# One core, four blocks in a row: gathers, combining and reflections moved to other places in the instruction order

## The chip, the cores and the metric

The program runs on one core of a Trainium2 chip. The metric is the device time of one execution in microseconds (us), from launch to end, and the figure quoted for a kernel is the median of its runs. A core has five engines that run their own instruction streams in order and meet through semaphores: PE (matrix products), DVE (vector), ACT (scalar functions), POOL (vector work of a slower kind, and all indirect DMA here) and SP (which only starts DMAs in this kernel). A wait of one instruction therefore holds everything that stands behind it on the same engine.

## What is computed

The input x is 4 x 512 x 288 in float32, the condition 4 x 288. Four blocks follow each other: a transformer block whose MLP is a mixture of 4 experts (top 2), a plain transformer block, a rotation in a 64-dimensional subspace, and another plain transformer block. The parts that the change touches come from the first and the third:

```python
# block 0: the expert MLP
topk_logits, topk_idx = jax.lax.top_k(xf @ w_gate, 2)
gates = jax.nn.softmax(topk_logits, axis=-1)
cw = jnp.sum(jax.nn.one_hot(topk_idx, 4) * gates[..., None], axis=1)
hmid = gelu(jnp.einsum('tc,ech->eth', xf, w1) + b1[:, None, :])
eo = jnp.einsum('eth,ehc->etc', hmid, w2) + b2[:, None, :]
x = x + g_mlp[:, None, :] * jnp.einsum('te,etc->tc', cw, eo)
...
# block 2: rotation; it needs only P and the condition until x arrives
U, _ = jnp.linalg.qr(P)                      # P is 288 x 64
R = _rotation(cond, W, b)                    # expm of a 64 x 64 skew matrix per batch
z = jnp.einsum('btn,nd->btd', x, U)
x = x + jnp.einsum('btd,nd->btn', jnp.einsum('btd,bde->bte', z, R) - z, U)
```

## The kernel before

**The order is written out by hand.** Each block is an attention stage followed by an MLP stage. Inside a stage, Python code issues the products of PE one by one, and other work is hung between them: generators are advanced with `next`, and lists of steps are run at fixed places. What is issued earlier stands earlier in each engine's stream. `in_turn(engine, ins)` ties an instruction behind the last one so tied on its engine and takes its place; `take` only takes the place; `beside_of` only ties.

**The expert stage.** Tokens are sorted by expert into 19 items of 256 rows, each the work of one expert (items 0 to 18; item 0 is done at the end of the attention stage). An item has 9 chunks: `hidden` computes four chunks at a time (products of 256 columns into `e0h`, then a gelu on ACT), and `contraction` multiplies by the second weights (two row tiles of 9 products of 288 columns into `e0o`). `others` alternates one group of four chunks with a stretch of the contraction of the item before. Behind each of these steps `breathe()` (L1940) is called once. After a group, `event(i, f)` (L1947) runs what was planned for its chunks.

The weights of an item depend on the sorting, so POOL gathers them by indirect DMA, all through `gathered` (L1815, the instruction of L1818): three first parts (`first_part`, 128 rows of 1,155 floats out of `w1c`), three second parts (`second_part`, 128 rows of 864 floats out of `in_w`, and with the first of them one bias gather), and two gathers of tokens (`tokens_of`). In `finish` (L1953) these are planned per chunk: second part n of item i at chunk n, first part n of item i+1 at chunk 3+n, the tokens of item i+2 at chunks 6 and 7, and at chunk 5 the transposes of item i+1 (`activations`, tile `e0xt`).

From item 12 on, `combining` brings the results of the first two batches back: per tile t of 128 tokens two gathers out of `eo` (`fetched`), two weightings and an addition on DVE, and an addition to x on POOL (L1936). It is planned at chunks, tile t seven chunks after tile t-1. A second list, `self.fine`, holds small pieces of the sorting of the other two batches; `breathe` takes one of them every fourth call.

**The side work.** `tick()` (L772) advances a generator of side work by one step, from the list `beside`; with `both=True` it advances the list `aside` as well, in that order. `beside` starts with `rotation()`: 64 Householder reflections (`reflections`, L579), then 64 steps that build the subspace (`subspace`). `aside` starts with `exponential()` (56 steps: loads and products `psr`, their evacuation `rv`, the matrix `skew`, a Taylor series, 16 squarings `ef`), behind which the modulation of block 1 is put (16 steps, with the tiles `rows` and `psmod`). In an attention stage four ticks fall on each of the 17 rounds; in the expert stage `went` counts the columns that PE streamed and ticks once per `pace` columns, 985 here, with `both`.

One reflection is a chain: on DVE a sum of squares and `n2` (L606), on POOL a square root `nrm` (L609), on DVE six small operations (L614 to L619), then an SP DMA that spreads one row of `pT` over up to 63 partitions (`reflector`, L545, tile `v`), and at last `reflect` on DVE, whose first instruction is the copy of L549. Between them stand the `yield`s, that is, the ticks: after `n2` (L608), after the square root (L610), two after the DMA, and in attention stages one after `reflect`.

## Time and profile before

| | |
|---|---|
| median of 3 runs | 2022.97 us (2016.03, 2022.97, 2024.35) |
| the profiled execution | 2016.98 us |
| its span, first to last instruction | 2015.0 us |
| PE busy | 1913.5 us (95%) |
| DVE, ACT, POOL busy | 1076.7, 746.6, 539.9 us |
| mean granted PE clock | 0.975 |
| attention of block 0, about | 30 to 410 us |
| expert stage, about | 410 to 925 us |
| attention and MLP of block 1, about | 925 to 1460 us |
| rotation, block 3 | 1460 us to the end |

The stages follow from the names of the tiles in the timeline; their bounds are read off where the first and last of these names stand. In the answers quoted below, a line of the waits reads: engine, who waited, for what; total us, how often, the longest. A line of the timeline reads: start us, length us, engine, line, operation, output<-inputs, count, and in brackets the idle time before it and who ended it. A float32 product shows as two records, so x18 stands for nine products.

### The profile page before, as it was taken

What the parts mean: (1) busy time and instruction counts of PE and PEld (TensorE: products, weight loads), DVE (VectorE), ACT (ScalarE), POOL (GpSimd) and SP (SyncE); (2) the same over time, 40 slices, a digit from 0 to 9 for tenths busy, and PEclk for the clock granted to TensorE, in tenths of its full rate; (3) what the DMA queues carried; (4) which work ended last, traced back from release to release, by engine and by line L of the source; (5) the groups of instructions that cost most, each with busy time, mean ns of one, the idle gap of its engine ahead of it and who ended that gap; (6) DMA issues with size and microseconds to landing.
All of it is one profiled execution on the core that took longest, in us unless ns stands there. A gap on an engine that the chain in (4) does not pass through costs nothing. (4 is left out here: it accounts for less than half of the span.)

```text
span 2015.0 us, 28809 instructions
## 1 busy us (share of the span) xinstructions
PE 1913.5 (95%) x10602; PEld 1008.9 (50%) x10602; DVE 1076.7 (53%) x3129; ACT 746.6 (37%) x1367; POOL 539.9 (27%) x776
## 2 busy tenths in 40 slices
PE   7999999998889899899999999999999999999998
PEld 4434443365556667675334443456554344433555
DVE  5666777623434333446777777454155666554211
ACT  1554555332211222232555544511124555555220
POOL 4111121443233445652332122211400211213101
PEclk9999999898889999899999999999999999999999
DMA  7521121346444665651111111220000111111000
GB/s 155 118 54 21 22 45 46 106 117 195 138 138 148 197 203 179 187 183 37 42 44 38 36 37 40 56 61 21 21 1 10 28 29 36 28 26 23 19 15 24
DMA packets 95166, 147.27 MB, mean 73 GB/s; under 512 B 33267, under 2 KB 72798, under 8 KB 95026
## 3 DMA queue, kind: packets, MB, share of 16 engines
q1 hardware_dynamic: 68690, 66.16, 14.3%
q0 software_dynamic: 26224, 79.27, 13.2%
q8 instruction: 84, 1.38, 0.3%
q14 instruction: 56, 0.46, 0.1%
q10 hardware_dynamic: 112, 0.01, 0.0%
HBM read 114.66 MB, written 20.54 MB: 67 GB/s over the span
## 5 line engine op out<-in xcount | busy, mean ns | idle before, releaser
L875 DVE TENSOR_REDUCE max<-a3m 128x1 f32<-128x512 f32 x256 | 164.6, 685 | 128.1 <-PE a3s L78 120.8
L78 PE MATMUL e0h<-e0hT,e0w 128*128 128x256 f32 (+1 forms) x1026 | 213.6, 416 | 13.1 <-DMA e0w<-w1c,wrow 10.2
L875 DVE TENSOR_REDUCE max<-a0m 128x1 f32<-128x512 f32 x256 | 165.3, 683 | 90.2 <-PE a0s L78 78.1
L875 DVE TENSOR_REDUCE max<-a1m 128x1 f32<-128x512 f32 x256 | 165.7, 684 | 75.3 <-PE a1s L78 68.0
L887 ACT ACTIVATE a0p<-a0s 128x512 f32<-128x512 f32 x256 | 140.2, 596 | 144.5 <-PE a0s L78 144.1
L887 ACT ACTIVATE a1p<-a1s 128x512 f32<-128x512 f32 x256 | 140.9, 596 | 139.4 <-PE a1s L78 139.2
L887 ACT ACTIVATE a3p<-a3s 128x512 f32<-128x512 f32 x256 | 140.0, 596 | 137.6 <-PE a3s L78 137.6
L78 PEld LDWEIGHTS e0h<-e0hT,e0w 128*128 128x128 f32 (+1 forms) x1026 | 149.6, 196 | 70.0 <-issue 47.2
L78 PE MATMUL e0o<-e0w,e0hm 128*128 128x288 f32 x648 | 178.6, 427 | 0.1
L78 PE MATMUL a0m<-a0qk,a0qk 32*128 32x512 f32 x512 | 159.1, 645 | 7.9 <-DVE max L875 6.8
L78 PE MATMUL a1m<-a1qk,a1qk 32*128 32x512 f32 x512 | 157.5, 640 | 7.8 <-DVE max L875 6.5
L78 PE MATMUL a0s<-a0qk,a0qk 32*128 32x512 f32 x512 | 161.0, 653 | 0.0
L78 PE MATMUL a1s<-a1qk,a1qk 32*128 32x512 f32 x512 | 158.4, 640 | 0.2 <-DVE u L549 0.2
L78 PE MATMUL a3m<-a3qk,a3qk 32*128 32x512 f32 x512 | 151.2, 643 | 6.8 <-DVE max L875 5.5
L78 PE MATMUL a3s<-a3qk,a3qk 32*128 32x512 f32 x512 | 153.0, 644 | 0.3 <-DVE a3qk L929 0.3
L78 PEld LDWEIGHTS e0o<-e0w,e0hm 128*128 128x128 f32 x648 | 125.5, 198 | 37.3 <-issue 2.7
L1281 ACT ACTIVATE e0hm<-e0h,e0w 128x256 f32<-128x256 f32 x162 | 75.6, 473 | 181.6 <-PE e0h L78 138.8
L609 POOL TENSOR_TENSOR nrm<-n,phalf 64x1 f32<-64x1 f32 (+31 forms) x64 | 36.4, 569 | 321.6 <-DVE n L606 296.4
L78 PEld LDWEIGHTS a1m<-a1qk,a1qk 32*128 32x128 f32 x512 | 46.9, 183 | 73.2 <-DVE max L875 41.1
L78 PEld LDWEIGHTS a0m<-a0qk,a0qk 32*128 32x128 f32 x512 | 47.3, 184 | 69.2 <-DVE max L875 41.2
L549 DVE COPY v<-v 63x1 f32<-63x1 f32 (+62 forms) x63 | 8.8, 139 | 134.5 <-DMA v<-pT 122.0
L78 PE MATMUL f1h<-f1hT,w 128*128 128x512 f32 (+1 forms) x216 | 79.9, 614 | 0.4 <-ACT f1hT L504 0.4
(496 smaller groups left out, 3241.1 us busy)
## 6 DMA issues: line engine op xcount, KB each, us to landing
eo<-e0r SPq DMA_DIRECT2D x50, 144.0 KB
ada<-in_ada SPq DMA_DIRECT2D x18, 324.0 KB
wr<-in_wrot SPq DMA_DIRECT2D x16, 288.0 KB
g<-gates SPq DMA_DIRECT2D x24, 144.0 KB
xm<-e0m SPq DMA_DIRECT2D x6, 576.0 KB
w1c<-in_w SPq DMA_DIRECT2D x20, 144.0 KB
w<-in_w SPq DMA_DIRECT2D x6, 432.0 KB
x<-in_x SPq DMA_DIRECT2D x16, 144.0 KB
```

Of the source, the lines that this page charges most:

```text
L78: ins = nc.tensor.matmul(*args, **kwargs).ins
L549: beside_of("DVE", nc.vector.tensor_copy(v[0:n, 0:1], v[0:n, C - k : C - k + 1]))
L609: in_turn("POOL", nc.gpsimd.tensor_tensor(nrm, n2, phalf[0:n], ALU.pow))
L875: take("DVE", nc.vector.tensor_reduce(m[:, t, i, D : D + 1], ps, AX.X, ALU.max))
L887: take("ACT", nc.scalar.activation(p, ps, AF.Exp, scale=D**-0.5))
L1281: nc.scalar.activation(self.hms[i][f], ps[r][:, 0 : self.width], func, bias=b1(f)),
```

## The change

Four edits, all in the order of issue; no arithmetic and no transfer is added or taken away.

1. In `reflections`, the `yield` between `n2` and the square root and the one after `reflect` in attention stages are removed: a reflection takes three ticks in every stage, where it took five in an attention stage and four in the expert stage.
2. In the expert stage `pace` is 1500 columns, where it was 985.
3. The gathers of an item form one list, made behind chunk 0: tokens of item i+1 (for two items only), the first parts of item i+1, the second parts of item i, the tokens of item i+2. `breathe` takes one behind every third call. What must be there by chunk 5 is taken at once then, the rest at chunk 8.
4. The combining is put into `self.fine`: a list made behind chunk 0 of item 12, with five steps of four `breathe`s to a tile.

```diff
@@ reflections
             nc.vector.tensor_scalar(sgn, alpha, 0.0, 2.0, ALU.is_ge, ALU.mult)
-            yield
             in_turn("POOL", nc.gpsimd.tensor_tensor(nrm, n2, phalf[0:n], ALU.pow))
             yield
...
                 reflect(k, pT, v, n - 1)
-                if inside[0]:
-                    yield
@@ Experts
-        pace, both = 985, True
+        pace, both = 1500, True
...
-        def breathe(self, every=4):
+        def breathe(self):
             self.since += 1
-            if self.fine and self.since >= every:
-                self.since = 0
+            if self.gathers and self.since % 3 == 0:
+                self.gathers.pop(0)()
+            if self.fine and self.since % 4 == 0:
                 self.fine.pop(0)()
@@ finish
-            tokens(2, 1, 1)
+            def gather(i):
+                self.gathers = []
+                if i + 1 in (2, NF0):
+                    self.gathers += self.tokens_of(i + 1)
+                if i < last:
+                    for n in range(FW):
+                        self.gathers.append(lambda n=n: self.first_part(i + 1, n))
+                for n in range(FW):
+                    self.gathers.append(lambda n=n: self.second_part(i, n))
+                self.urgent = len(self.gathers) - FW
+                if i + 2 <= last and i + 2 != NF0:
+                    two = []
+                    self.gathers += [
+                        lambda: (two.extend(self.tokens_of(i + 2)), two[0]()),
+                        lambda: two[1](),
+                    ]
+                self.later = len(self.gathers) - self.urgent
+            def gathered(left):
+                while len(self.gathers) > left():
+                    self.gathers.pop(0)()
             for i in range(1, self.items):
-                for n in range(FW):
-                    at(i, n, lambda i=i, n=n: self.second_part(i, n))
-                    if i < last:
-                        at(i, FW + n, lambda i=i, n=n: self.first_part(i + 1, n))
-                if i + 2 <= last and i + 2 != NF0:
-                    tokens(i + 2, i, 6)
+                at(i, 0, lambda i=i: gather(i))
+                at(i, 5, lambda: gathered(lambda: self.later))
+                at(i, 8, lambda: gathered(lambda: 0))
...
-            tokens(NF0, NF0 - 1, 0)
-            for t in range(HT):
-                k = (NS + 1) * NF + 2 + 7 * t
-                at(*divmod(k, NF), lambda t=t: self.fetched(0, t))
-                steps = combining(0, t)
-                for f, step in zip((6, 7, 8), steps):
-                    at(*divmod(k + f, NF), step)
+            def combine():
+                steps = [[] for _ in range(5 * HT + 4)]
+                for t in range(HT):
+                    steps[5 * t].append(lambda t=t: self.fetched(0, t))
+                    for k, step in zip((4, 5, 7), combining(0, t)):
+                        steps[5 * t + k].append(step)
+                self.fine = [lambda some=some: both(*some) for some in steps]
+            at(NS + 1, 0, combine)
+            at(last - 1, 4, placed)
```

Here NF = 9 chunks, FW = 3, NS = 11, NF0 = 5, HT = 8 and `last` = 18.

More of the change, by code (lines that the diff above doesn't have):

```diff
@@ L1438, in __init__ @@
             self.eo = [kept(f"eo{h}", [n * SW, C]) for h, n in enumerate((NS, NS1))]
-            self.fine, self.since = [], 0
+            self.fine, self.gathers, self.since = [], [], 0
             def pair(tag, shape, dtype=F32):
@@ L1982, in finish @@
             last = self.items - 1
-            def tokens(i, where, f):
-                steps = []
-                at(where, f, lambda: (steps.extend(self.tokens_of(i)), steps[0]()))
-                at(where, f + 1, lambda: steps[1]())
             for n, load in enumerate(loads):
                 at(NS // 2 + n, 4, load)
-            tokens(2, 1, 1)
-            for i in range(1, self.items):
-                for n in range(FW):
-                    at(i, n, lambda i=i, n=n: self.second_part(i, n))
-                    if i < last:
-                        at(i, FW + n, lambda i=i, n=n: self.first_part(i + 1, n))
-                if i + 2 <= last and i + 2 != NF0:
-                    tokens(i + 2, i, 6)
+            def gather(i):
[18 more added lines that the diff above has]
+                    self.gathers.pop(0)()
+            for i in range(1, self.items):
+                at(i, 0, lambda i=i: gather(i))
+                at(i, 5, lambda: gathered(lambda: self.later))
+                at(i, 8, lambda: gathered(lambda: 0))
                 if i < last:
```

## The prediction

> **What bounds the kernel.** I read the page first, then the waits of PE by stage, then the timeline around the long ones.

> ```profile
> PE 1913.5 (95%) x10602; PEld 1008.9 (50%) x10602; DVE 1076.7 (53%) x3129; ACT 746.6 (37%) x1367; POOL 539.9 (27%) x776
> ...
> PE   7999999998889899899999999999999999999998
> ...
> PEclk9999999898889999899999999999999999999999
> ```

> PE sets the time, and where it falls short (slices 8 to 17, 50 us each) its clock is low too. From the granted clock and PE's busy stretches I summed both over the expert stage (430 to 935 us): PE idle 48.7 us, and 30.1 us lost where it ran at half clock. That, 79 us, is all the change can win there. By part, idle + clock: 36.8 + 22.4 up to 700 us, while `aside` still works, and 11.9 + 7.7 after it. The waits of 420 to 930 us:

> ```profile
> POOL nrm L609 <- DVE n L606: 160.2, 35, 15.5
> ...
> DVE v L549 <- DMA v<-pT: 120.8, 30, 10.0
> ...
> PE e0h L78 <- DMA e0w<-w1c,wrow: 10.2, 3, 4.5
> ...
> POOL e0w L1818 <- PE e0o L78: 8.3, 3, 4.8
> ...
> PE psmod L410 <- DVE rows L397: 7.2, 2, 4.5
> ...
> PE e0xt L78 <- DVE rv L684: 5.9, 1, 5.9
> ...
> PE e0xt L78 <- DVE skew L717: 4.3, 1, 4.3
> ```

> A chain: DVE stands at the head of `reflect` until tile `v` lands; n2 follows it, so POOL stands at the square root, and the gathers behind it stand too. PE suffers in two ways. While `aside` works, its PSUM banks are emptied by DVE behind that wait (`rv`, `skew`, `rows`, `ef`, `m`: eight gaps of over 1 us, 24.6 us together). Later, three gathers of first weights come late:

> ```profile
> 747.52 0.71 PE L78 MATMUL e0h<-e0hT,e0w 32*128 32x256 f32 x6
> 752.17 7.02 PE L78 MATMUL e0h<-e0hT,e0w 32*128 32x256 f32 x18 [3.94 <-DMA e0w<-w1c,wrow]
> ...
> 762.03 4.37 PE L78 MATMUL e0h<-e0hT,e0w 32*128 32x256 f32 x24
> ```

> PE waits 3.94 us and then needs 7.02 us for 18 records that cost 4.37 x 18/24 = 3.28 us elsewhere. So a gap costs almost twice its length.

> [...] The trace has 13 half-clock stretches of 3.4 to 10.2 us in this stage, several behind gaps of 1 to 3 us, and 30.1 us lost. [...]

> **Ticks.** Columns: 162 chunks x 2 x 256 = 82,944 and 18 items x 2 x 9 x 288 = 93,312, together 176,256. Before 176,256/985 = 179 ticks, after 176,256/1500 = 117.5. Attention 0 leaves 63 ticks to the reflections: before 63/5 = 12.6, then 179/4 = 44.7, so 57 at the end of the experts. The trace has the 58th copy of `v` at 941 us: the count holds. After: 63/3 = 21, then 39, 60 in all. `aside` needs 72 ticks: the first 40% of the stage before, 61% after.

> **Part 1 and 2, in the expert stage.** Between the issue of `v` and its copy lie two ticks: 1970 columns before, 3000 after. Nine products of 288 columns took 4.53 us (801 us), so 1.75 ns a column: 1.8 us more; with all other work of the stage (472 us over 179 ticks, 2.64 us each; after, some 440/117.5 = 3.74) it is 2.2 us more. The 33 waits of this stage (133.3 us with those laid to issue) lose 2.1 us each where they have it: about 67 us remain, half. The eight PE gaps shrink likewise to 0, 3.8, 2.1, 0.8, 0, 0, 2.4, 0.6 = 10 us, but 24 reflections now fall into `aside`'s time instead of 18: 13 us. Lower end: all 24.6 go; upper end: only the 1.8 us of full clock each, times 24/18: 15 remain. I take **-12 us**, and of the 22.4 us clock loss the same share of idle (12/36.8): **-7 us**. The wait `psr` for its load (2.5 us, once) has half again as long to land: **-2**.

> The chain's own length also matters once `aside` is done: landing 3.3 to 5 us, 2.1 to n2, 0.75 to the square root and 1.1 to the next issue make 7.3 to 9; PE's pure columns allow 3940 x 1.75 = 6.9 us before, 7.9 after. Less room was missing than is now given, so the chain need no longer hold POOL behind PE.

> The square root moved one tick up now stands before the gathers of that tick, which wait for n2 with it. It costs nothing while those gathers have lead (next part); it never ran before n2 anyway.

> **Part 3, the gathers.** Each gather occupies POOL 0.95 us + 0.30 issue. Numbers stay; places change. First part 0 of item i+1 was issued behind the group with chunk 3. Where a group of four straddles items as [.. i:2 to 5][6,7,8, i+1:0] this leaves 9 calls of `breathe` (0.52 us each at 38 calls per 20 us item): 4.7 us, while the three late ones took 6.8, 4.6 and 5.5 us from issue to use. After, it goes 3 calls behind chunk 0's group: 18 to 24 calls, 9 to 12 us. The three waits (10.2) and their clock (7.7) should go: 0 to -17.9, I take **-16**. Second parts are issued 12 to 18 calls later than before; the tightest alignment leaves 12 calls to its contraction and six products more for the third, 9.4 us against 6.8: hidden, with 2.6 us to spare. If the cover goes, `e0o` waits in place of `e0h`. They stand behind the first parts on POOL, and no longer before them; that removes `POOL e0w <- PE e0o` from in front of the first parts. Item 2's tokens come 3 us before their transposes: **+2 us**, once. Tokens of others keep over 20 calls.

> [...]

> **Part 4, combining.** The 16 gathers, 16 weightings, 8 additions on DVE and 8 on POOL spread over 44 x 4 = 176 calls, 4.6 items instead of 6.2: POOL per item 9 + 3.5 gathers (15.6 us), 1.7 additions (0.8 each) and 2.3 roots (0.75): 18.7 us of a 20 us item; before 9 + 2.6: 17.5. Still below, but no cover is left for a stop. The first weighting comes 16 calls, 8 us, behind its gather. Taken at **0**; up to a gap of 7.7 us an item if POOL falls behind.

> **Part 1 in attention stages.** 8.4 more reflections in attention 0, 3.0 us of DVE each (L549 to L619: 0.14 + 0.49 + 0.15 + 0.47, 0.5 + 0.35, 6 x 0.15), 25 us over 350 where DVE is 72% busy. PE's waits there:

> ```profile
> PE a0m L78 <- DVE max L875: 6.8, 10, 1.6
> ```

> Block 3's attention, with no reflections, has 5.5 us of the same wait, so 1.3 us go to 12.6 reflections: **+1 us**, at most 4.5. `v` still has two ticks of 5 us. Block 1's side work ends 22 ticks earlier; nothing waited for its end.

> **Sum:** -12 - 7 - 2 - 16 + 2 + 1 = -34 us. The profiled execution took 2016.98 us, so 1983; it lies 6 us under the median of the runs shown and 1 us above the lowest. I say **1985 us**.

> **Rivals.**
> - *POOL becomes the bound* (slower). In items 12 to 18, at 18.7 of 20 us, an addition waiting on DVE, or a root waiting for n2, pushes the next first weights past their use: seven gaps like that at 843 us (4.5 + 3.2 clock) = +54, while the three old ones go (-18) and part 1 and 2 gives -21: 2032 us. It decides from about 1.3 us of lost POOL time an item. For: POOL's waits at n2 total 160 us. Against: those waits arise when POOL is ahead. 18% here, and 3% for other losses.
> - *Second weights wait instead*: -21 + 3, and the 18 us come back at `e0o`, with late roots adding as much: about 2015, no change. 10%.
> - *DVE's stops persist*, since `aside` meets 24 reflections: only the first weights are won: -16 + 3 gives 2004. 14%.
> - *Everything goes*: spreading also shortens `v`'s landing, all 24.6 + 10.2 us go and two thirds of the 30 us clock loss: 1963. 12%.
> - That the steps do not come as said: POOL may issue gathers in bursts behind each root, not by threes. They run ahead then, which harms nothing in the sum.

> The forecast itself (1972 to 1998) has 43%.

> **How the numbers follow.** About 0.5% (10 us) is what the measurement can tell from no change. Faster: 43 + 12 + 14 = 69%, less 1 for its edge = 68; same 10 + 1 = 11; slower 21. The range runs from under the best case, 1956, to the POOL case, 2034; outside lie some 15 to 20%.

> **What would show it.** Right: no `e0h` waiting for `w1c`; `DVE v <- DMA v` in the experts at half or less; the `e0xt` and `psmod` gaps below 14 us; fewer half-clock stretches; the 21st reflection at the stage's start. Wrong: `e0o` waiting for a DMA, or POOL without idle time from item 12 on with PE gaps there; longer `a0m <- max` waits above 12 us.

## The result and the profile after

The changed kernel takes 2001.13 us in the median of 4 runs (1994.04 to 2007.69); the kernel before had 2023.37 us in 4 runs (2016.03 to 2024.35). The ratio is 0.9893, interval 0.9864 to 0.9922: 1.1% faster, 22 us. The profiled execution of the changed kernel was the longest of its four, 2007.69 us with a span of 2005.6 us. It stands 9.3 us below the profiled execution before.

This is the page of the changed kernel: busy time by engine, then, in 40 slices of 50 us, PE's busy tenths and the granted clock.

```profile
PE 1913.5 (95%) x10602; PEld 1006.4 (50%) x10602; DVE 1079.8 (54%) x3129; ACT 748.5 (37%) x1367; POOL 540.6 (27%) x776
...
PE   7999999998889989999999998999999999999998
...
PEclk9999999989899989998999999999999899999999
```

PE's busy sum is the same to a tenth. In slices 8 to 17 (counted from 0), the expert stage, fewer are below 9 in both rows. But a clock of 8 now also stands in slice 18, where attention 1 begins, and in slice 31. The sum hides what moved. I cut both traces at the first product of each stage (`a0m`, `e0h`, `a1m`, `f1h`, `rt`):

| us (lost to half clock in brackets) | attention 0 | experts | attention 1 | MLP 1 | all later |
|---|---|---|---|---|---|
| before | 375.7 (9) | 519.3 (34) | 361.3 (2) | 173.9 (2) | 555.0 |
| after | 390.5 (10) | 480.0 (19) | 373.7 (9) | 170.7 (0) | 559.9 |
| difference | +14.8 | -39.3 | +12.4 | -3.2 | +4.9 |

"Lost to half clock" is half the length of the stretches in which the trace grants half speed. The expert stage won 39.3 us: PE's idle time fell by 16.3 us (48.9 to 32.6), its busy time at half clock cost 15.2 us less (30.1 to 14.9), and 7.7 us came out of time that shows as busy. Two thirds of the 39.3 us went back in the two attention stages. The +4.9 us of "all later" are half clock too (4 us before, 9 after). (The rest to the 9.4 us of the spans is 1 us ahead of the first product.) The table compares two single executions, 9.3 us apart, where the medians are 22 us apart; so it tells where time moved, and not to the microsecond how much.

The waits of the stage (420 to 930 us) in the changed kernel. Columns: engine and line, what it waited for, us in all, times, longest.

```profile
POOL nrm L608 <- DVE n L606: 167.5, 32, 11.4
...
DVE v L549 <- DMA v<-pT: 94.9, 26, 8.8
...
PE psmod L410 <- DVE rows L397: 6.8, 1, 6.8
...
PE e0o L78 <- DMA e0w<-in_w,wrow: 5.5, 3, 3.6
...
PE e0xt L78 <- DVE m L725: 3.7, 1, 3.7
...
PE e0h L78 <- DMA e0w<-w1c,wrow: 1.0, 1, 1.0
```

The first weights (`w1c`) are no longer late: 1.0 us for 10.2. Part of it has passed to the second weights (`in_w`, 5.5 us), which were never late before. DVE's wait for `v` fell from 120.8 to 94.9 us only, and POOL's for n2 not at all; neither of these is a wait of PE.

Attention 0 is harder to see. These are two rows of one stretch of 280 us in it, of the kernel before and of the changed one. Columns: the stretch, its length, then busy us (and instructions) of PE, its weight loads, DVE, ACT and POOL, then the granted clock, the share of DMA and GB/s.

```profile
60.00:340.00 280.00, 276.06 (x1759) 117.26 (x1759) 201.12 (x477) 143.30 (x257) 55.19 (x93) 1.00 0.22 46
```

```profile
60.00:340.00 280.00, 272.36 (x1670) 115.70 (x1668) 209.04 (x546) 137.55 (x245) 57.76 (x97) 0.99 0.23 46
```

PE is busy 1.3% less, but it completed 5.1% fewer records of products (1670 for 1759) in the same time. The page shows it for one product of this stage, before and after. Behind the bar stand the busy time of all and the mean time of one in ns:

```profile
L78 PE MATMUL a0m<-a0qk,a0qk 32*128 32x512 f32 x512 | 159.1, 645 | 7.9 <-DVE max L875 6.8
```

```profile
L78 PE MATMUL a0m<-a0qk,a0qk 32*128 32x512 f32 x512 | 167.5, 648 | 13.1 <-DVE max L872 10.7
```

One product takes as long as before, but the 512 together cover 8.4 us more: they overlap less. So look at the counts, since products that follow each other less closely still look like a busy PE. DVE has 69 instructions more in this stretch: some 80 more of the reflections, and a dozen fewer of the attention's own.

### The profile page after: what moved, and what is told of

The parts are those of the page before. It is cut to its first block, busy times and chain, and to the rows that moved or that the text cites. A ratio compares the mean times of both kernels' runs of the same rounds, so it can differ in the third digit from the quotient of the medians.

```text
span 2005.6 us, 28759 instructions
## 1 busy us (share of the span) xinstructions
PE 1913.5 (95%) x10602; PEld 1006.4 (50%) x10602; DVE 1079.8 (54%) x3129; ACT 748.5 (37%) x1367; POOL 540.6 (27%) x776
## 3 DMA queue, kind: packets, MB, share of 16 engines
q0 software_dynamic: 26224, 79.27, 13.2%
## 5 line engine op out<-in xcount | busy, mean ns | idle before, releaser
L78 PE MATMUL e0h<-e0hT,e0w 128*128 128x256 f32 (+1 forms) x1026 | 198.5, 407 | 2.2 <-DMA e0w<-w1c,wrow 1.0
L78 PE MATMUL e0o<-e0w,e0hm 128*128 128x288 f32 x648 | 178.8, 427 | 10.1 <-DMA e0w<-in_w,wrow 5.5
L78 PE MATMUL a0m<-a0qk,a0qk 32*128 32x512 f32 x512 | 167.5, 648 | 13.1 <-DVE max L872 10.7
L78 PE MATMUL a1m<-a1qk,a1qk 32*128 32x512 f32 x512 | 165.2, 647 | 9.6 <-DVE max L872 8.4
L78 PE MATMUL a0s<-a0qk,a0qk 32*128 32x512 f32 x512 | 169.2, 656 | 0.0
L78 PEld LDWEIGHTS e0h<-e0hT,e0w 128*128 128x128 f32 (+1 forms) x1026 | 142.4, 191 | 52.9 <-issue 31.8
L78 PE MATMUL a1s<-a1qk,a1qk 32*128 32x512 f32 x512 | 163.7, 645 | 0.2 <-DVE u L549 0.2
L78 PE MATMUL a3m<-a3qk,a3qk 32*128 32x512 f32 x512 | 152.1, 647 | 6.8 <-DVE max L872 5.5
L78 PE MATMUL a3s<-a3qk,a3qk 32*128 32x512 f32 x512 | 153.5, 647 | 0.2 <-DVE a3qk L926 0.2
L78 PEld LDWEIGHTS e0o<-e0w,e0hm 128*128 128x128 f32 x648 | 124.3, 197 | 48.7 <-ACT e0hT L1878 6.9
L78 PEld LDWEIGHTS a0m<-a0qk,a0qk 32*128 32x128 f32 x512 | 49.5, 185 | 80.8 <-DVE max L872 46.8
L78 PEld LDWEIGHTS a1m<-a1qk,a1qk 32*128 32x128 f32 x512 | 50.3, 186 | 78.2 <-DVE max L872 42.4
L78 PE MATMUL f1h<-f1hT,w 128*128 128x512 f32 (+1 forms) x216 | 79.9, 614 | 0.0
L78 PE MATMUL f3h<-f3hT,w 128*128 128x512 f32 (+1 forms) x216 | 79.4, 613 | 0.4 <-ACT f3hT L504 0.4
```

The lines of the kernel that those rows point to most:

```text
L78: ins = nc.tensor.matmul(*args, **kwargs).ins
```

## The experiments

All are edits of the changed kernel. Their stages, in us as above, how many reflections (copies of `v`) fall into attention 0, experts, later, and in the last column attention 0 and attention 1 less what was lost to half clock:

| | attention 0 | experts | attention 1 | MLP 1 | reflections | less half clock |
|---|---|---|---|---|---|---|
| before | 375.7 | 519.3 | 361.3 | 173.9 | 12 / 45 / 6 | 367.1 / 359.6 |
| after | 390.5 | 480.0 | 373.7 | 170.7 | 20 / 39 / 4 | 380.3 / 365.2 |
| later yield back | 379.0 | 485.6 | 367.9 | 169.5 | 15 / 39 / 9 | 370.5 / 357.7 |
| the same, again | 382.6 | 485.6 | 364.6 | 169.5 | 15 / 39 / 9 | 367.2 / 357.7 |
| earlier yield back | 386.9 | 478.5 | 375.7 | 168.8 | 15 / 39 / 9 | 376.7 / 363.8 |
| none in attention 0 | 369.6 | 495.2 | 378.4 | 196.5 | 0 / 39 / 24 | 361.1 / 366.4 |
| dead work added | 420.8 | 480.3 | 376.5 | 171.0 | 20 / 39 / 4 | 395.2 / 368.0 |
| old gathers | 392.7 | 497.8 | 371.8 | 170.8 | 20 / 39 / 4 | 380.7 / 365.0 |
| 985 columns | 395.9 | 536.6 | 396.8 | 160.8 | 20 / 43 / 0 | 378.8 / 372.9 |
| old combining | 392.3 | 478.4 | 372.5 | 170.8 | 20 / 39 / 4 | 380.3 / 364.0 |
| both yields, 1300 | 378.8 | 500.9 | 364.2 | 169.6 | 12 / 45 / 6 | 368.6 / 359.1 |
| later yield, 1700 | 376.8 | 466.4 | 361.0 | 170.0 | 15 / 35 / 13 | 368.3 / 355.9 |
| 2 ticks in attention 1 | 379.5 | 486.3 | 353.5 | 188.2 | 15 / 39 / 9 | 367.5 / 353.5 |

Four kernels with the changed attention (after, old gathers, 985, old combining) give 390.5 to 395.9 us in attention 0, and four with the later yield 376.8 to 382.6: a difference of 5 us in one stage of one profile says nothing. Most of this scatter is half clock, which falls differently in each execution (8.5 and 15.4 us in the two profiles of one kernel, the later yield back). Without it the first four give 378.8 to 380.7 us and the second four 367.2 to 370.5.

**One yield back.** What costs the attention stages their 27 us? Either the number of reflections (20 for 12) or their packing, several pieces in one tick. Both kernels here have 15 in attention 0, four ticks each, and differ in which pieces share a tick. The first has the yield after `reflect`:

```diff
                 reflect(k, pT, v, n - 1)
+                if inside[0]:
+                    yield
```

> The yield after reflect is put back for attention stages: four ticks per reflection there, three among the experts, so 15.75 reflections in block 0's attention instead of 21. Stage from the first a0m to the first e0h: 375.7 us in the profile of before (12.6 reflections), 390.6 after (21). Theory 'amount' (each reflection's DVE work costs PE a fixed time in attention): 15.75 reflections give 375.7 + 3.15 x 1.8 = 381, and block 1's attention falls back from 374 towards 365; the whole about 1985. Theory 'burst' (the seven DVE operations in one tick are what hurts): the stage falls by more, to about 376, since reflect and the next sum of squares are in different ticks again. Theory 'accident' (one collision in round 12, 5 us, and scatter): no clear change, 388 to 391.

The second has the yield before the square root, so `reflect` and the dots of the next stay together:

```diff
+            if inside[0]:
+                yield
             in_turn("POOL", nc.gpsimd.tensor_tensor(nrm, n2, phalf[0:n], ALU.pow))
```

> The yield between n2 and the square root is put back for attention stages only; also four ticks per reflection and 15.75 reflections in block 0's attention, but reflect and the next sum of squares stay in one tick (seven DVE operations). Theory 'amount': the same 381 us for the stage as with the other yield put back, and about 1985 in all. Theory 'burst': no fall, 388 or more. Theory 'accident': 388 to 391.

The later yield: 1985.26 us in 4 runs, ratio to before 0.9792 (0.976 to 0.9824), 1% better than the changed kernel; a repeat of it gave 1987.11 us, 0.9822 (0.9778 to 0.9867), 0.7% better. The earlier yield: 1999.47 us, 0.9877 (0.9837 to 0.9918), which is the changed kernel's time. Attention 0 came to 379.0 and 382.6 us with the later, 386.9 us with the earlier. PE's wait for the maxima in attention 0, of the changed kernel, then with the later yield, then with the earlier:

```profile
PE a0m L78 <- DVE max L872: 10.7, 14, 2.0
```

```profile
PE a0m L78 <- DVE max L874: 7.1, 10, 1.5
```

```profile
PE a0m L78 <- DVE max L874: 10.6, 13, 1.9
```

With 15 reflections each, the one that keeps `reflect` and the next dots together waits as the changed kernel does with 20, and without half clock its attention 0 takes 376.7 us where the four with the later yield take 367.2 to 370.5. So the packing costs, not only the number. Of the two expectations for the earlier yield, 381 (amount) and 388 or more (burst), the 386.9 us lie nearer the second. That the place of the pieces within a round does it is unlikely: with four ticks to a round and four to a reflection the pieces stand at the same places in every round, with three they wander, and both packed kernels pay about the same for a reflection (below). In the trace of the changed kernel DVE works off such a tick as follows (start, us, engine, line, operation, out and in):

```profile
297.65 0.69 DVE L926 TENSOR_TENSOR a0qk<-a0qk,a0sh 128x512 f32<-128x512 f32 x1 [0.26 <-PE a0sh L78]
298.25 0.14 DVE L549 COPY v<-v 50x1 f32<-50x1 f32 x1
298.43 0.44 DVE L555 CUSTOM_DVE_ANT_0 junk<-pT,v 50x275 f32<-50x275 f32 x1
...
298.80 0.68 DVE L872 TENSOR_REDUCE max<-a0m 128x1 f32<-128x512 f32 x1
...
299.57 0.50 DVE L573 SCALAR_TENSOR_TENSOR pT<-v,w,pT 50x275 f32<-50x275 f32 x1
300.11 0.44 DVE L555 CUSTOM_DVE_ANT_0 junk<-pT 50x273 f32<-50x273 f32 x1
...
300.54 0.67 DVE L872 TENSOR_REDUCE max<-a0m 128x1 f32<-128x512 f32 x1
```

From 297.65 to 301.21 us DVE has hardly a rest (3.46 of 3.56 us busy), and two maxima that PE waits for run 1.74 us apart with pieces of a reflection between them.

**None in attention 0, and more of it.** In the first, attention 0 no longer takes ticks for the reflections; in the second each reflection in an attention stage brings three operations of 64x288 whose result nobody reads:

```diff
...
-                    tick()
+                    side()     # l > 0, or work that must come first: tick()
...
```

> Block 0's attention ticks only for its own modulation, so not one or at most one reflection stands there; the reflections left over run later, some without cover at the end of block 1's MLP, so the whole gets longer (2040 to 2120 us) and says nothing. Theory 'amount': the stage a0m to e0h falls to 390.6 - 21 x 1.8 = 353 us, the 352.6 of block 3's attention, which has no side work. Theory 'accident' or other causes (routing, modulation): it stays at 375 or more.

```diff
                 reflect(k, pT, v, n - 1)
+                if inside[0]:
+                    for m in range(3):
+                        nc.vector.scalar_tensor_tensor(
+                            junk, pT[:, 0:C], 1.0, pT[:, 0:C], ALU.mult, ALU.add)
```

> Behind each reflect in an attention stage three more DVE operations of 64 x 288, about 0.48 us each, whose output nothing reads; 1.44 us more DVE work per reflection (3.0 before), 21 of them = 30 us in block 0's attention. Theory 'amount', at 0.6 us of PE time per us of DVE work (1.8 for 3.0): the stage grows by 18 us to about 409. If only the count of reflections or their waits matter (POOL's root, the landing of v): 391. Whole run 2000 + 18 + 3 = 2022 against 2004.

Without reflections: attention 0 369.6 us, the whole 2026.57 us in one run, since 24 of them now run behind the expert stage; the experts take 15.2 us more and MLP 1 25.8. Attention 0 was expected to fall to the 353 us of attention 3, which has no side work. It didn't: of the 23 us between these two in the kernel before, the reflections are 6. With dead work: attention 0 420.8 us (409 expected), the whole 2034.14 us in one run. The same stretch of attention 0 with the later yield, and with dead work:

```profile
60.00:340.00 280.00, 275.36 (x1733) 117.43 (x1733) 205.37 (x512) 143.26 (x255) 56.01 (x94) 1.00 0.22 49
```

```profile
60.00:340.00 280.00, 266.41 (x1563) 110.42 (x1561) 206.18 (x532) 128.51 (x227) 51.90 (x87) 0.96 0.21 43
```

DVE is no busier with dead work (206 us for 209), and yet PE completes 1563 records for 1670. DVE is idle for a quarter of the stretch in both, so it is not that DVE is full. The costliest groups of DVE have the dead operations with (after the bar) 32.9 us busy in all and 457 ns each, for the 24 reflections in both attention stages:

```profile
L627 DVE SCALAR_TENSOR_TENSOR dead<-pT 64x288 f32<-64x288 f32 x72 | 32.9, 457 | 1.4
```

Those of the 20 reflections in attention 0 are 60 x 0.457 = 27.4 us, and the stage grew by 30.3 us; about half of these is half clock (26 us lost for 10), and 15 us are left without it. Now all kernels against the one without reflections, less half clock (361.1 us, one profile): 12 reflections in five ticks (two kernels) cost 6.0 and 7.5 us, 0.5 to 0.6 each; 15 in four with the later yield (four kernels, mean 368.4) 7.3, 0.5 each; 15 with the earlier 15.6, 1.0; 20 in three (four kernels, mean 380.0) 18.9, 0.9. So a reflection in separate pieces costs about 0.5 us and a packed one about 1. Number and packing both count: by this estimate 8 reflections more at 0.5 us are 4 us, a third of what attention 0 lost, and 20 times 0.45 us for packing are 9, two thirds.

**The gathers.** Edit 3 undone, all else as changed:

```diff
...
-                at(i, 0, lambda i=i: gather(i))
-                at(i, 5, lambda: gathered(lambda: self.later))
-                at(i, 8, lambda: gathered(lambda: 0))
...
+            tokens(2, 1, 1)
...
+                for n in range(FW):
+                    at(i, n, lambda i=i, n=n: self.second_part(i, n))
+                    if i < last:
+                        at(i, FW + n, lambda i=i, n=n: self.first_part(i + 1, n))
...
```

> The changed kernel with the third edit undone: gathers planned at their chunks again (second part n at chunk n, first part n of the next item at chunk 3+n). The expert stage (first e0h to first a1m) took 480 us in the changed kernel, 519 before. Theory of the prediction: the three late first weights come back, 10 us of waits for w1c and 8 us of clock, so the stage takes about 496 us and the whole about 2017. Rival: with ticks of 1500 columns the first weights are no longer held, so nothing comes back (478 to 485 us), and the gathers were worth nothing.

2019.16 us in 10 runs, ratio 1.0005 (0.9981 to 1.0029): without it the change is worth nothing. The expert stage takes 497.8 us, 17.8 more than with edit 3. Three long waits in PE's timeline of this kernel (start, us, tiles, count, and in brackets the wait ahead), one for the tokens of item 2 and two for first weights:

```profile
470.51 1.92 PE L78 MATMUL e0xt<-ident,e0xs 128*128 128x128 f32 x19 [6.24 <-DMA e0xs<-xm,token]
...
808.71 7.05 PE L78 MATMUL e0h<-e0hT,e0w 32*128 32x256 f32 x20 [5.58 <-DMA e0w<-w1c,wrow]
...
838.90 7.29 PE L78 MATMUL e0h<-e0hT,e0w 32*128 32x256 f32 x18 [8.28 <-DMA e0w<-w1c,wrow]
```

The first weights are later than before the change (4.5 us at most), and the products behind them again run at half speed: 7.29 us for 18, where 24 took 4.37 us in the kernel before. The tokens are late here and neither in the kernel before nor in the changed one: the new ticks with the old gathers bring a wait of their own. So the 17.8 us are what edit 3 is worth beside the other edits, and not the first weights alone.

**The distance of the ticks, and the combining.** First `pace` alone back, then edit 4 alone undone:

```diff
-        pace, both = 1500, True
+        pace, both = 985, True
```

> The changed kernel with 985 columns to a tick again, reflections in three ticks: the reflections end among the experts (179/3 = 60), and the subspace starts there. Theory of the prediction (two ticks of 985 columns are too short for v to land, and aside hangs on that): the stage of 480 us takes about 500, DVE waits for v of 95 us rise to 150 or more, and the gaps of PE at e0xt and psmod come back. Rival (the ticks' distance is worth nothing, the gathers did it all): 480 to 486. Block 0's attention stays at 390.

```diff
...
-            at(NS + 1, 0, combine)
-            at(last - 1, 4, placed)
...
+                at(*divmod(k, NF), lambda t=t: self.fetched(0, t))
...
+                for f, step in zip((6, 7, 8), steps):
+                    at(*divmod(k + f, NF), step)
```

> The changed kernel with the fourth edit undone, the combining planned at its chunks again. The prediction took the edit at 0, so 480 us for the expert stage, within 5. If the fine steps help, 485 to 490; if POOL was driven near its bound by them, 470 to 475. Whole 1996 to 2006.

At 985 columns: 2066.39 us, ratio 1.0241 (1.0208 to 1.0274). The expert stage takes 536.6 us, 57 more, and attention 1 23 more. The waits of this kernel from 410 to 940 us:

```profile
DVE v L549 <- DMA v<-pT: 118.3, 38, 8.3
...
PE e0h L78 <- DMA e0w<-w1c,wrow: 13.1, 3, 8.1
PE e0o L78 <- DMA e0w<-in_w,wrow: 10.1, 7, 3.2
...
PE psmod L410 <- DVE rows L397: 9.8, 2, 8.4
```

With three ticks to a reflection and the old distance DVE meets 38 waits for `v` instead of 26 (118 us of them, where 150 or more were expected), and both kinds of weights come late, though edit 3 is in: three ticks need the longer distance. It also packs all other side work of `aside` closer, so it isn't a measure of the reflections alone. The combining: 2002.0 us, 0.9934 (0.9903 to 0.9964; before took 2018.76 us on that chip), experts 478.4 us for 480.0, no difference clear of the noise.

**Where it leads.** Both yields in attention stages with a distance between; the later yield with a still longer distance (and MLP 1's own, 750 for 1000, to hold what is left over); and, for attention 1, half its ticks (and MLP 1's distance 640):

```diff
-        pace, both = 1500, True
+        pace, both = 1300, True     # and both yields under inside[0]
```

> The changed kernel with both yields of a reflection put back in attention stages only (five ticks there, three among the experts) and 1300 columns to a tick, so that the side work still ends under cover: 12.6 + 45 reflections by the end of the experts. Theory 'burst' (a reflection in small pieces costs block 0's attention about 0.5 us, in one piece 1.05): the stage a0m to e0h takes 375 to 378 us instead of 390, the expert stage 480 to 486, the whole about 1980 to 1986, at or under the 1985 with one yield. Theory 'amount' at 1.8 us each: also 375, so this run does not tell the two apart; it looks for a better version.

> The kernel with the yield after reflect put back in attention stages once more, as the measure for the two runs beside it: 1985 us, ratio 0.979 to before as in its first run, if that was no luck of the chip; block 0's attention 377 to 381 us, the expert stage 480 to 487.

```diff
-        pace, both = 1500, True
+        pace, both = 1700, True     # and the later yield
...
-        pace = 1000
+        pace = 750
```

> That same kernel with 1700 columns to a tick among the experts instead of 1500 and 750 instead of 1000 in the plain MLPs, so that the side work still ends under cover. Theory of the tick's distance (two ticks must outlast v's landing and what aside needs; 536 us at 985, 501 at 1300, 480 to 486 at 1500): the expert stage takes 472 to 480. Rival (1500 is past the knee): no gain, 482 to 488. Block 1's attention has 13.7 reflections instead of 9 and grows by 2 to 5. Whole 1978 to 1990.

```diff
-    attention(1, w, feed.mod, 1e-6, feed, 4, hT=hT, also=also)
+    attention(1, w, feed.mod, 1e-6, feed, 2, hT=hT, also=also)     # the later yield, pace 640
```

> That same kernel with two ticks instead of four in each round of block 1's attention and 640 columns to a tick in the MLP behind it, where DVE is nearly idle. If it is the side work on DVE that lengthens block 1's attention (361 us before, 368 with the yield, 374 in the changed kernel, against 350 in block 3), it falls to 356 to 360 and the MLP grows by less than 3 from 170: whole about 1975 to 1980. If its length is the clock's doing (half-clock stretches early in it), it stays at 365 to 368.

1300 with five ticks: 2006.3 us in 10 runs, 0.9941 (0.9909 to 0.9973), where 1980 to 1986 were expected. It keeps attention 0 and 1 low (378.8, 364.2), but the experts take 500.9 us, and not 480 to 486.

**1700 with the later yield is the fastest kernel here: 1970.05 us in 5 runs (1958.5 to 1976.12), ratio to before 0.9741 (0.9686 to 0.9795).** Its profile is of the fastest of the five, 12 us under their median, so its stages are a little flattered. Experts 466.4 us, attention 0 and 1 as before the change. The stage fell below the 472 to 480 us that were expected. Its waits there (410 to 890 us):

```profile
DVE v L549 <- DMA v<-pT: 74.9, 18, 15.5
...
PE e0o L78 <- DMA e0w<-in_w,wrow: 4.0, 2, 3.6
...
PE e0h L78 <- DMA e0w<-w1c,wrow: 0.8, 1, 0.8
```

Two ticks in attention 1: 1992.71 us, 0.9842 (0.9786 to 0.9898), no better than four. Attention 1 does fall by 11 to 14 us, to 353.5, with no half clock in it. But MLP 1, which was to grow by less than 3 us, takes 188.2 us, since the work it has now taken over comes late; PE stands there for the last reflection:

```profile
PE psue L753 <- DVE uT L573: 8.8, 1, 8.8
```

## Why the prediction was right, and where it was not

The direction was right: 22 us of 34 foreseen, in the medians. (The 34 us were taken from the profiled execution; from the median before they give 1989.) 2001 us lies 3 us above the range that the forecast gave itself, 1972 to 1998, and nearest to the 2004 of the rival *DVE's stops persist*. DVE's stops did persist, but that rival let the expert stage win 13 us, and it won 39.3, where the forecast's terms for it add up to 35. The rest was lost in the attention stages. Step by step:

- **The first weights, -16: right.** Edit 3 alone is worth 17.8 us in the expert stage, with the wait for the tokens of item 2 in them. The waits for `w1c` went (10.2 to 1.0 us) and, in its absence, come back (14.3 us, three times).
- **Part 1 and 2 in the expert stage (-12 idle, -7 clock, -2 `wr`, +2 tokens: -19): right as a sum, and not by the mechanism.** The stage won 39.3 us; less 17.8 leaves 21.5. The eight gaps of `aside`'s work that were to shrink from 24.6 to 13 us did so: four over 1 us are left, 13.2 us together. But they were to shrink because each wait for `v` lost 2.1 us, half in all. These waits lost a fifth (120.8 to 94.9 us), and while `aside` works, where the gaps lie, all the idle time ahead of the copies of `v` is 51.5 us for 54.0 (up to 700 us before, up to 730 us after). So that 13 us came out is luck as far as the argument goes. That PE is spared because the steps of `aside` now have more products between them is likely, and not shown. The 7.7 us out of time that shows as busy had no term at all. And the step from 985 columns to 1500 is worth 57 us with three ticks to a reflection, where the two parts together were given 19: at 985 columns three ticks take 536.6 us even with edit 3, more than the 519.3 us of four ticks without it, and the distance wins that back. The prediction priced the two edits together, and so didn't see that one costs what the other must win back.
- **The signs named for the stage: all but one right.** Half-clock stretches fell from 13 to 6, 20 copies of `v` lie ahead of the stage as counted, and the `psmod` and `e0xt` gaps sum to 13.9 us where under 14 was asked (6.8 and 3.7 are the large ones). The tokens of item 2, +2, didn't show. The wait for `v` at half or less is the one that missed.
- **Second weights hidden with 2.6 us to spare: too sure.** They wait 5.5 us, three times. The rival built on it (18 us) did not come.
- **The rival *Everything goes*: no.** By it the spreading of the gathers also shortens the landing of `v`. In the kernel before, `v` was there 2.0 us after its issue at 916 us (7 rows, the gathers over) and 9.6 us after the issue at 793 us (21 rows, among gathers). But where DVE waits for it in the expert stage, issue to copy took 4.3 us in the mean of 33 before and 4.5 in the mean of 26 after.
- **POOL as the bound, combining at 0: right.** The late first weights of that rival, seven times 4.5 us, did not come (1.0 us, once), and the old combining is 2002.0 us against 2001.1.
- **Part 1 in attention stages, "+1 us, at most 4.5": this is the step that failed.** Attention 0 took 14.8 us more, attention 1, which the prediction passed over with "nothing waited for its end", 12.4. Without these 27.2 us the pair of profiles would lie 36.5 us apart, close to the 34 of the forecast. The step took what a reflection costs PE from one line, the wait of PE for the maxima (6.8 us, and 5.5 without reflections), and this line hides most of it: it rose to 10.7 us, 3.9 more and under the 12 that were named as a sign of error. Of the 14.8 us of attention 0, all idle time of PE is 6.0, half clock 1.7, and 7.1 are products that follow each other less closely and show as busy. It also took 0.1 us for a reflection (1.3 us for 12.6), where about 0.5 us were measured in separate pieces, and gave no term to packing, which makes it about 1. What would have shown it: the counts of products by stretch, and the stage's own length without reflections. The length of attention 3 (352.6 us) would have misled the other way, since only 6 us of its 23 us to attention 0 are the reflections'.

How it came about, by the 16 rounds of attention 0 (16 maxima each), in us:

| round | 7 | 9 | 11 | 12 | 13 | 14 |
|---|---|---|---|---|---|---|
| before | 21.4 | 22.2 | 22.7 | 22.9 | 22.2 | 21.4 |
| after | 22.2 | 22.5 | 24.0 | 23.3 | 27.3 | 23.8 |
| later yield | 21.4 | 21.4 | 22.7 | 22.9 | 22.2 | 22.5 |
| earlier yield | 23.0 | 23.0 | 24.1 | 23.4 | 22.5 | 23.8 |
| none | 21.2 | 21.4 | 22.0 | 22.9 | 22.1 | 21.4 |

With the earlier yield rounds 7, 9 and 11 are 1.4 to 1.6 us longer than with the later one at the same number of reflections. These rounds repeat: the four kernels with the later yield have the same 21.4, 21.4 and 22.7 us, the four with three ticks 22.2 or 22.3, 22.5 and 24.0. Round 13 of the changed kernel is something else: there the routing of the first tokens meets a reflection on DVE, and POOL's additions. It cost 5.1 us here, half clock included, and 3.4 to 6.4 us in the three other kernels with the changed attention; with 15 reflections it doesn't appear.

**What stays open.** In attention 1 the changed kernel loses in rounds 1 and 2 (21.4 and 24.0 us for 17.8 and 22.2) and in round 5 (27.3 for 21.4), each with a half-clock stretch; no other is more than 0.8 us longer. So 6.8 of its 12.4 us are half clock, which another execution may not have (next section but one). Without it the stage takes 365.2 us for 359.6, and in the table this splits the kernels as in attention 0: 357.7 us twice with the later yield, 363.8 with the earlier, 364.0 and 365.0 with the old combining and the old gathers. Why is not clear, for only 4 reflections of `v` are there; those of tile `u`, which come after all of `v`, begin 74 us into the stage, and 181 us in the kernel before. That the side work as a whole makes this is shown by the kernel with half the ticks (rounds 17.8, 22.2, 21.4, 20.9 and 21.3 us); which part of it, the reflections, the norms or the end of the combining, was not separated. Two kernels weren't tried: five ticks in the attention stages with 1700 columns in the experts, and four ticks among the experts with 1500, which would show whether three ticks win anything there.

## What to carry to other kernels

Work that was slipped in beside a bound engine had two prices here: how much of it there is (about 0.5 us of attention 0 for a reflection in separate pieces), and how much lies between two things that engine waits for (about 1 us for a packed one). So cut such work into pieces, and lengthen the distance where the pieces themselves wait for a transfer (1500 columns for 985 took 57 us off the expert stage). When a step is given to a stage in which "nothing waits", price it by that same stage's length with and without such work, less half clock, and by counts of products in equal stretches, not by PE's busy share, by one wait row, or by another stage that lacks more than this work. A gather or load is best placed by how long before its use it is issued, and both neighbours need to be checked, as the ones behind it become the late ones (here the waits for first weights fell from 10.2 to 1.0 us, and those for second weights came up, 5.5 us).

## What the hardware showed that was not expected

**Half clock also follows gaps of under 1 us, and PE's being busy does not end it at once.** Three adjoining stretches in attention 1 of the changed kernel (columns as above; the clock is the third figure from the end):

```profile
992.00:995.30 3.30, 2.53 (x10) 0.94 (x10) 3.27 (x6) 1.11 (x3) 2.57 (x4) 0.94 0.77 226
995.30:1002.10 6.80, 6.80 (x29) 1.20 (x26) 3.00 (x12) 1.21 (x3) 1.01 (x2) 0.53 0.14 41
1002.10:1005.40 3.30, 3.30 (x18) 2.03 (x19) 3.30 (x8) 2.52 (x5) 1.83 (x4) 1.00 0.22 47
```

A gap of 0.77 us at 993.9 us, the longest near it, is followed by 6.83 us of half clock in which PE is busy throughout. At 1564.9 us there are 10.24 us of half clock, all of them busy, with no gap over 0.76 us in the seven us ahead. Such gaps are not always followed by it. These are two stretches of 15 us at the start of round 5 of attention 1, with the same products at their start and the same two gaps (0.76 and 0.97 us; 0.77 and 0.96 us), first of the kernel before, then of the one with both yields and 1300 columns:

```profile
1024.00:1039.00 15.00, 13.27 (x86) 5.38 (x79) 10.45 (x26) 7.93 (x14) 4.62 (x9) 1.00 0.13 19
```

```profile
1008.50:1023.50 15.00, 13.27 (x58) 4.73 (x54) 8.51 (x22) 5.23 (x9) 0.79 (x1) 0.66 0.09 11
```

In the expert stage after the change half clock cost 14.9 us of PE's busy time, in six stretches. Three begin in PE's longest gaps or at their end (6.8, 3.7 and 3.6 us, at 714.9, 597.6 and 824.0 us). The other three come behind shorter ones: at 465.8 us after 1.0 us, at 489.7 after 2.3, and at 530.7 after 2.4 (in one of 1.3). Gaps of 1.7 us at 471.4 and of 2.2 at 513.1 have none behind them for 15 us. So a hold-up of about 1 us can be followed by a loss of several: behind the 0.77 us above, 6.83 us at half clock are 3.4 us lost.

**A small DVE operation took six times its usual length.** In round 13 of attention 0, in the changed kernel's DVE timeline:

```profile
301.46 0.23 DVE L2088 TENSOR_TENSOR e0r0ahead<-e0r0lg 128x64 f32<-128x64 f32 x1
301.60 1.36 DVE L2089 TENSOR_TENSOR e0r0tie<-e0r0lg 128x64 f32<-128x64 f32 x1
```

Two operations on the same tile of the same size. During the second POOL runs a square root (301.48 us, 0.62 us) and an addition of 128x288 (302.09 us, 0.78 us). Over the changed kernel's trace additions and comparisons of this form take 0.51 us in the mean of the 6 that POOL's arithmetic overlaps, this one among them (1.36 us, one of 0.83, four of 0.21 to 0.23), and 0.22 us in the 10 others. That POOL's work is the cause was not tried by itself.
